# The order of matrix-product pieces on TensorE in a two-layer graph network kernel, and one PSUM read moved on VectorE

## The chip, the cores and the metric

The kernel runs on one core of a Trainium2 chip. The metric is device time in microseconds for one execution. Before the change it is 2293.26 us, the median of 3 runs (2292.56 to 2294.22).

## The reference: what is computed

The input x has 128 graphs of 128 nodes with 512 features. Two layers follow each other, each with a layer norm and a ReLU ahead of it and a residual sum behind it. All of it is in float32.

```python
h = relu(layernorm(x));  x = x + (norm_adj @ (h @ W0)) + b0
h = relu(layernorm(x))
q, k, v = h @ Wq + bq, h @ Wk + bk, h @ Wv + bv            # 8 heads of 64
attn = softmax(q k^T / 8 + (1 - adj) * -1e9)               # per graph and head
x = x + (attn @ v) @ Wo + bo
```

So there are five 512 x 512 weight products: W0, Wq, Wk, Wv and Wo.

## The kernel before, in words

Four graphs form a group, 32 groups in all. In the steady state a turn of the main loop (slot `t`) runs five blocks, named by a letter: W (the product with W0 for group t+1), Q, K, V (the products with Wq, Wk, Wv for group t) and Y (the product with Wo for group t-1). Each block is one `Projection` of seven steps, `n` = 0 to 6. Between the steps, and between the two halves of a step (`step(n)`, then `rest(n)`), a table called `plan` puts everything else: layer norms, transposes, scores, softmax, loads and stores. The schedule is manual: each engine works through its instructions in the order in which the program issues them. An instruction waits on semaphores for what it needs from other engines.

**Fewer multiplications.** A product of two 512 x 512 blocks is done in seven half-size products, P1 to P7 (the Winograd form of Strassen's scheme). Four of these, P2 to P5, are themselves split into seven pieces, each a 128 x 128 by 128 x 128 multiplication; P1, P6 and P7 are plain, four multiplications of 128 x 256 each. The sums of pieces are not made on TensorE: VectorE (in a few places ScalarE) reads each PSUM bank and adds it into the right blocks of the destination in SBUF.

**PSUM banks.** P1, P6 and P7 use one of the two `a` banks. P5 and later P3 use the two `d` banks: the seven pieces lie as four blocks in `d0` and three blocks in `d1` (`SEVEN`, `seven`, lines 403 to 411). P2 uses bank `b` and P4 bank `c`; each of the two is filled in three phases of 4, 2 and 1 pieces (`PHASES`, `phase`), because the sums allow a phase's places to be read, and then added to, by the next phase.

**The seven steps.** 0: P1. 1: P5 into `d0`, `d1`. 2: P2's phase of four into `b`. 3: P6. 4: P2's phase of two, then P3 into `d0`, `d1` on top of P5. 5: P7. 6: P2's last piece and P4's phase of four into `c`. P4's last two phases, of two pieces and of one, are put off: they go to a list, `tail`, and run within steps 1 and 2 of the following block. They are the trailing phases. Block K is an exception (`whole`): its P4 runs inside the block, with its first phase in step 4 ahead of P3, its second at the start of step 5, and its third in step 6. So W's trailing phases run in Q, Q's in K, V's in Y and Y's in W; V runs none.

**Reads on VectorE.** The bank of a phase is read by `read_phase`. The `d` banks are read by `read_seven`: part 0 reads the first two blocks of `d0` (in Q, K and V for P5 this is done by ScalarE), and then the first block of `d1` onto the diagonal; part 1 is four reads, the last of `d1` second and the last of `d0` fourth. Part 0 for P5 is issued in `rest(1)`, part 1 in `rest(2)`; for P3 both are in `rest(4)`. P3 writes on the same banks, so its first multiplication waits until P5 is read. Likewise a phase of `c` or `b` waits until the phase before it is read.

**What else stands in VectorE's queue.** The statistics of the layer norms (`BATCH_NORM_STATS2`, line 314) are put by the plan at "Q0b", "Q1b" and "Q3b" (the group's x just loaded) and at "K0b" and "K3b" (the second norm). "K3b" lies between P5's reads and those of step 4 in block K.

Of the kernel before, what the change touches and what calls it, by code (L numbers as in the profile page):

```python
# [29 lines left out]
P1, P5, P2, P6, P3, P7, P4 = PRODUCTS = (  # L30
    (A11, W11),
    (S1, T1),
    (A12, W21),
    (S2, T2),
    (S4, W22),
    (S3, T3),
    (A22, T4),
)
# [40 lines left out]
SEVEN = ((3, 6, 0, 0), (0, 5, 0, 1), (2, 3, 0, 2), (1, 0, 0, 3), (4, 4, 1, 0), (5, 2, 1, 1), (6, 1, 1, 2))  # L79
# [14 lines left out]
def kernel(  # L94
# [18 lines left out]
    P = 128  # L113
# [151 lines left out]


    INNER = [((T1, W22), step) for step in FIRST_RIGHT[:3]]
    INNER += [((W21, T4), WINOGRAD_RIGHT[0])]
    INNER += [((T1, W22), step) for step in FIRST_RIGHT[3:]]
    INNER += [((W21, T4), step) for step in WINOGRAD_RIGHT[1:]]  # L270

    def combine_inner(name, engine, steps=range(9)):
# [103 lines left out]
    class Projection:  # L376
# [23 lines left out]
                    else:  # L400
                        self.matmul(out[:, r], left[:, c, r, :], right[:, c, :], start)

        def seven(self, product, fresh):
            i, k = product
            for x, y, b, place in SEVEN:
                self.matmul(
                    bank[f"d{b}"][:, place * P : (place + 1) * P],
                    self.left.slot(i, x),
                    self.right.slot(k, y),
                    fresh and place == 0,  # L410
                )
# [35 lines left out]
        def read_seven(self, half, y, part, first=False):  # L447
            dst = self.cut(half, y)
            diagonal = self.diagonal(dst)
            m = [bank[f"d{b}"].rearrange("p (s f) -> p s f", f=P) for b in range(2)]  # L450
            columns = m[0][:, 0:2].unsqueeze(2).to_broadcast([P, 2, 2, P])
            if part == 1:
                self.add(dst[:, 1, 0], m[0][:, 3])
                self.add(diagonal, m[1][:, 1:3])
                self.add(dst[:, 0, 1], m[0][:, 2])
                self.add(diagonal, m[0][:, 2:4], ALU.subtract)
                return
            if first and self.first is not None:
                self.first(dst.rearrange("p j r f -> p r j f"), columns, y)
            else:  # L460
                self.add(dst.rearrange("p j r f -> p r j f"), columns)
            self.add(diagonal, m[1][:, 0:1].to_broadcast([P, 2, P]))

        def read_phase(self, half, y, src, n):
            dst, m = self.cut(half, y), src.rearrange("p (s f) -> p s f", f=P)
# [9 lines left out]
        def step(self, n):  # L475

            a, inner = bank[f"a{turn[0]}"], self.inner
            t, m = self.region(1, 0), bank["c"]
            left = tail.pop(0) if n in (1, 2) and tail else None
            if left:  # L480

                left[0]()
            if n == 0:
                self.left, self.right = self.a(), w_sb[self.w]
                self.product(a, P1, True)
                self.read_first(0, 0, a)
            elif n == 1:
                if inner:
                    self.seven(P5, True)
                else:  # L490
                    self.product(bank["d0"], P5, True)
            elif n == 2:
                if inner:
                    self.phase(bank["b"], P2, 0)
                else:
                    self.product(bank["b"], P2, True)
            elif n == 3:
                self.product(a, P6, False)
                self.read_first(0, 1, a)
            elif n == 4:  # L500
                if inner:
                    self.phase(bank["b"], P2, 1)
                    if self.whole:
                        self.phase(m, P4, 0)
                    self.seven(P3, False)
                    self.read_phase(0, 0, bank["b"], 1)
                    if self.whole:

                        self.whole(t[:, 0, :], m[:, : 2 * P], 0)
                        self.whole(t[:, 1, P:], m[:, 3 * P :], 1)  # L510
                        self.add(t[:, 0, :P], m[:, 2 * P : 3 * P])
                else:
                    self.product(bank["d0"], P3, False)
            elif n == 5 and self.whole:
                self.phase(m, P4, 1)
                self.product(a, P7, False)
                self.whole(t[:, 1, :P], m[:, 3 * P :], 1)
                self.add(t[:, 1, :P], m[:, :P])
                self.add(t[:, 0, :], a[:, : 2 * P])
                self.add(t[:, 1, P:], a[:, 3 * P :])  # L520
                turn[0] = 1 - turn[0]
            elif n == 5:
                self.product(a, P7, False)

                reads = [lambda: self.read_first(1, 0, a), lambda: self.read(1, 1, a)]
                for f in reads if self.stay else reads[::-1]:
                    f()
                turn[0] = 1 - turn[0]
            elif self.whole:
                self.phase(bank["b"], P2, 2)  # L530
                self.phase(m, P4, 2)
                self.read_phase(0, 0, bank["b"], 2)
                a = bank[f"a{1 - turn[0]}"]
                self.add(t[:, 1, :P], a[:, 2 * P : 3 * P])
                self.read(1, 1, a)
                self.read_phase(1, 0, m, 2)
            elif inner:
                self.phase(bank["b"], P2, 2)
                self.phase(bank["c"], P4, 0)
                self.read_phase(0, 0, bank["b"], 2)  # L540
                self.read_phase(1, 0, bank["c"], 0)
                for k in (1, 2):
                    tail.append(
                        (
                            lambda k=k: self.phase(bank["c"], P4, k),
                            lambda k=k: self.read_phase(1, 0, bank["c"], k),
                        )
                    )
            else:
                self.product(bank["c"], P4, True)  # L550
                self.read(1, 0, bank["c"])
            if left:
                left[1]()
            if n == 2:
                if inner:
                    self.read_phase(0, 0, bank["b"], 0)
                else:
                    self.read(0, 0, bank["b"])

        def rest(self, n):  # L560

            inner = self.inner
            if n == 1:
                if inner:
                    self.read_seven(1, 1, 0, True)
                else:
                    self.read_first(1, 1, bank["d0"])
            elif n == 2 and inner:
                self.read_seven(1, 1, 1)
            elif n == 4:  # L570
                if inner:
                    self.read_seven(0, 1, 0)
                    self.read_seven(0, 1, 1)
                else:
                    self.read(0, 1, bank["d0"])
# [272 lines left out]
    for t in range(-1, NG + 1):  # L848
# [3 lines left out]
        if 0 <= t - 1 < NG - 1:  # L852
            g = t - 1

            for first, final, place, f, *args in (
# [14 lines left out]
                place = first if t == 1 else final if last else place  # L870
# [307 lines left out]
```

## Time and profile before

| | |
|---|---|
| median of the runs | 2293.26 us |
| profiled execution, span from first to last instruction | 2291.6 us |
| TensorE busy with matmuls | 2273.9 us, 99% |
| weight loads on TensorE busy | 2132.9 us, 93% |
| VectorE busy | 1868.3 us, 82% |
| ScalarE busy | 1364.3 us, 60% |
| GpSimd busy | 1860.9 us, 81% |
| DMA, share of 16 engines | 80.6% |
| mean granted TensorE clock | 0.998 |

The profiled execution has no time of its own beside its span; the span lies 1.7 us below the median of the runs. A steady turn of the loop takes about 70 us. Matmul ends are modelled, so that overlapping records hide short gaps: the busy share of 99% does not say how much of the time TensorE waits. What counts are the starts. In an undisturbed stretch a 128 x 128 multiplication shows as two records whose starts lie 112 ns apart, and a 128 x 256 one as two records 216 ns apart. A weight load stands ahead of each record.

### The profile page before, as it was taken

The numbers are of one execution on the slowest core, as the hardware profiler recorded it, in microseconds if no ns is written. First come the engines' busy times: TensorE is split into PE (matmuls) and PEld (weight loads), VectorE is DVE, ScalarE is ACT, GpSimd is POOL, SyncE is SP. The second block draws the span as 40 slices with busy tenths as digits, with TensorE's granted clock in tenths as the row PEclk, the third lists the DMA queues.
The fourth block names the chain that finished last, engine by engine and source line by source line (L and its number), as shares of the span: only waits on it lengthen the run. The fifth ranks groups of instructions, "written<-read, shape, count | busy, mean of one in ns | idle before, by whom it ended". The sixth has DMA issues, their size and how long they took to land.

```text
span 2291.6 us, 50617 instructions
## 1 busy us (share of the span) xinstructions
PE 2273.9 (99%) x18151; PEld 2132.9 (93%) x18151; DVE 1868.3 (82%) x4832; ACT 1364.3 (60%) x3556; POOL 1860.9 (81%) x1927
## 2 busy tenths in 40 slices
PE   9899999999999999999999999999999999999999
PEld 8899999999999999999999999999999999999998
DVE  7877888888888788887888888888888888888876
ACT  3555565655656556656556565565665665655654
POOL 6899788878888788888888887879888888878854
PEclk9999999999999999999999999999999999999999
DMA  5388978889887889878898788998888987889872
GB/s 169 157 259 245 298 231 256 239 251 280 250 252 241 254 254 276 257 247 236 251 297 243 250 238 250 270 258 260 244 246 252 291 253 236 243 245 291 239 242 81
DMA packets 448587, 563.32 MB, mean 246 GB/s; under 512 B 326352, under 2 KB 333648, under 8 KB 447824
## 3 DMA queue, kind: packets, MB, share of 16 engines
q1 hardware_dynamic: 448336, 560.08, 80.6%
q8 instruction: 144, 2.36, 0.4%
q14 instruction: 107, 0.88, 0.1%
HBM read 358.68 MB, written 122.68 MB: 210 GB/s over the span
## 4 chain that ended last, share of the span: by engine, by line
PE 88%; POOL 3%; DMA 3%; DVE 3%; issue 1%; ACT 1%; SPq 0%; POOLq 0%; DVEq 0%; ACTq 0%
PE bank_a L388 31%; PE bank_d L388 19%; PE bank_c L388 10%; PE bank_b L388 10%; PE pa L605 5%; PE bank_d L754 3%; PE po L820 3%; DMA xt<-in_x_dram 2%; PE pss L754 1%; PE bank_b L820 1%; PE bank_a L820 1%; PE bank_b L754 1%; PE pt L674 1%; POOL xt L337 1%; DVE xt L429 1%
## 5 line engine op out<-in xcount | busy, mean ns | idle before, releaser
L781 ACT ACTIVATE att<-att,nmx 128x128 f32<-128x128 f32 x1024 | 396.3, 391 | 0.9 <-DVE nmx L773 0.9
L388 PE MATMUL bank_a<-op_h,w 128*128 128x256 f32 x1488 | 352.0, 379 | 0.0
L789 POOL TENSOR_TENSOR att<-att,rsm 128x1024 f32<-128x1024 f32 x128 | 242.7, 1897 | 82.3 <-DVE rsm L788 82.3
L388 PEld LDWEIGHTS bank_a<-op_h,w 128*128 128x128 f32 x1488 | 268.9, 190 | 29.0
L429 DVE TENSOR_TENSOR xt<-xt,bank_d 128x512 f32<-128x512 f32 x732 | 269.0, 416 | 19.0 <-DVE xt L429 0.9
L794 ACT COPY att<-att 128x2048 uint16<-128x2048 uint16 x121 | 229.3, 1895 | 66.0 <-POOL att L789 66.0
L333 ACT ACTIVATE h<-xt,nb,rs 128x512 f32<-128x512 f32 x254 | 207.2, 817 | 57.8 <-POOL nb L322 56.1
L711 ACT ACTIVATE q<-bank_a,bqk 128x256 f32<-128x256 f32 x192 | 80.4, 470 | 263.0 <-PE bank_a L388 263.0
L320 POOL TENSOR_TENSOR rs<-ve,mhalf 128x2 f32<-128x2 f32 (+1 forms) x129 | 91.4, 708 | 176.2 <-DVE ve L319 175.8
L388 PE MATMUL bank_d<-op_h,w 128*128 128x128 f32 (+1 forms) x1712 | 218.2, 279 | 0.7 <-issue 0.3
L90 POOL TENSOR_TENSOR op_o<-op_o 128x256 f32<-128x256 f32 x297 | 209.6, 729 | 10.0
L388 PEld LDWEIGHTS bank_d<-op_h,w 128*128 128x128 f32 x1712 | 204.0, 193 | 5.1 <-issue 3.1
L90 POOL TENSOR_TENSOR op_a<-op_a 128x256 f32<-128x256 f32 x279 | 196.8, 729 | 14.1 <-DVE op_a L365 4.5
L90 POOL TENSOR_TENSOR op_h<-op_h 128x256 f32<-128x256 f32 x270 | 190.4, 729 | 12.2 <-DVE op_h L365 2.9
L781 ACT ACTIVATION_READ_ACCUMULATOR att<-att,nmx 128x1 f32 x1024 | 194.1, 190 | 0.0
L314 DVE BATCH_NORM_STATS2 st<-xt 128x6 f32<-128x512 f32 x256 | 173.0, 676 | 18.4 <-DMA xt<-in_x_dram 18.3
L388 PE MATMUL bank_a<-w,op_o 128*128 128x256 f32 x768 | 181.7, 379 | 0.0
L388 PE MATMUL bank_a<-w,op_h 128*128 128x256 f32 x744 | 179.1, 384 | 0.0
L388 PE MATMUL bank_a<-w,op_a 128*128 128x256 f32 x744 | 176.1, 380 | 0.0
L439 DVE TENSOR_TENSOR xt<-bank_a,xt 128x512 f32<-128x512 f32 x252 | 167.2, 684 | 10.2 <-PE bank_a L388 2.7
L761 DVE SCALAR_TENSOR_TENSOR att<-bank_d,msk 128x512 f32<-128x512 f32 x128 | 82.5, 686 | 104.4 <-PE bank_d L754 96.8
L773 DVE TENSOR_REDUCE nmx<-att 128x8 f32<-128x1024 f32 x128 | 155.0, 1211 | 0.0
(188 smaller groups left out, 5944.3 us busy)
## 6 DMA issues: line engine op xcount, KB each, us to landing
w<-wd_v SPq DMA_DIRECT2D x93, 704.0 KB, 5.5
w<-wd_o SPq DMA_DIRECT2D x93, 704.0 KB, 6.8
w<-wd_q SPq DMA_DIRECT2D x90, 704.0 KB, 6.1
planes<-att SPq DMA_DIRECT2D x121, 512.0 KB, 4.5
w<-wd SPq DMA_DIRECT2D x87, 704.0 KB, 5.4
xt<-in_x_dram SPq DMA_DIRECT2D x63, 512.0 KB, 6.1
out_dram<-xt SPq DMA_DIRECT2D x62, 512.0 KB, 4.2
planes_h<-att SPq DMA_DIRECT2D x29, 512.0 KB, 3.0
```

Of the source, the lines that this page charges most:

```text
L90: engine.tensor_tensor(twice(out), twice(x), twice(y), ALU.subtract if minus else ALU.add)
L314: nc.vector.bn_stats(self.st[:, j, :], self.src[:, j, :])
L333: nc.scalar.activation(h, src[:, j, :], AF.Relu, bias=nb[:, j : j + 1], scale=rs[:, j : j + 1])
L388: nc.tensor.matmul(out, lhsT, rhs, start=start, stop=True, skip_group_check=True)
L429: nc.vector.tensor_tensor(dst, dst, src, f)
L439: nc.vector.tensor_tensor(t, src.rearrange("p (r f) -> p r f", r=2), t, ALU.add)
L605: nc.tensor.matmul(pa[:, c * P : (c + 1) * P], h[:, c * P : (c + 1) * P], ant, start=True, stop=True)
L754: nc.tensor.matmul(pss[p][:, c, :], qs[g][rows, c, cols], ks[g][rows, c, cols], start=True, stop=True)
L773: nc.vector.tensor_reduce(nmx, att_of(g, b), AX.X, ALU.max, negate=True)
L781: nc.scalar.activation(att[:, h, :], att[:, h, :], AF.Exp, bias=nmx[:, h : h + 1], scale=1.0, accum_out=sm[:, h : h + 1])
L789: nc.gpsimd.tensor_tensor(att, att, rsm.unsqueeze(2).to_broadcast([P, H, P]), ALU.mult)
L794: nc.scalar.copy(planes, halves)
```

## The change

The multiplications, reads and other instructions are the same in number and kind; their order on TensorE and VectorE is not. ScalarE, GpSimd and the DMA queue have the same order as before.

- Step 1: the trailing phase of two is moved from ahead of P5 to between P5's four pieces in `d0` and its three in `d1`.
- Step 2: the trailing phase of one is moved behind P2's phase of four. On VectorE its read goes behind the two reads of `b`.
- Step 4: P3 starts with its three pieces in `d1`; its four in `d0` follow.
- `read_seven`: the read of the first block of `d1` moves from the end of part 0 to the start of part 1. For P5 this takes it from `rest(1)` to `rest(2)`, behind the reads of `b` and of the trailing phase. For P3 both parts stand together, so nothing moves.

```diff
-        def seven(self, product, fresh):
+        def seven(self, product, fresh, banks=(0, 1)):
             i, k = product
-            for x, y, b, place in SEVEN:
+            for x, y, b, place in (s for c in banks for s in SEVEN if s[2] == c):
...
             if part == 1:
+                self.add(diagonal, m[1][:, 0:1].to_broadcast([P, 2, P]))
                 self.add(dst[:, 1, 0], m[0][:, 3])
...
                 self.add(dst.rearrange("p j r f -> p r j f"), columns)
-            self.add(diagonal, m[1][:, 0:1].to_broadcast([P, 2, P]))
...
             left = tail.pop(0) if n in (1, 2) and tail else None
-            if left:
-
-                left[0]()
...
             elif n == 1:
                 if inner:
-                    self.seven(P5, True)
+                    self.seven(P5, True, (0,))
                 else:
                     self.product(bank["d0"], P5, True)
+                if left:
+                    left[0]()
+                if inner:
+                    self.seven(P5, True, (1,))
             elif n == 2:
                 if inner:
                     self.phase(bank["b"], P2, 0)
                 else:
                     self.product(bank["b"], P2, True)
+                if left:
+                    left[0]()
...
-                    self.seven(P3, False)
+                    self.seven(P3, False, (1, 0))
...
-            if left:
-                left[1]()
             if n == 2:
                 if inner:
                     self.read_phase(0, 0, bank["b"], 0)
                 else:
                     self.read(0, 0, bank["b"])
+            if left:
+                left[1]()
```

Here `left` holds a trailing phase: `left[0]` its multiplications, `left[1]` its reads.

## The prediction, made before the changed kernel was run

> **What bounds the kernel now.** I read the page first, then the chain, the waits, and the timeline of single engines.
>
> ```profile
> PE 2273.9 (99%) x18151; PEld 2132.9 (93%) x18151; DVE 1868.3 (82%) x4832; ACT 1364.3 (60%) x3556; POOL 1860.9 (81%) x1927
> PE 88%; POOL 3%; DMA 3%; DVE 3%; issue 1%; ACT 1%; SPq 0%; POOLq 0%; DVEq 0%; ACTq 0%
> ```
>
> TensorE sets the end, and the same multiplications remain. So the change can only take away, or add, short stops of TensorE. The view of waits of the weight loads shows one large one:
>
> ```profile
> PEld bank_c L388 <- DVE xt L429: 10.9, 16, 4.2
> ```
>
> Most stops are too short for that view. I took the start of every matmul record from the timeline; where a bank changes, what the first two starts lie apart beyond 112 ns (216 ns for a wide record) is a stop. All such stops come to 44 us. By place: second trailing phase of W, in Q: 6.9 us in 16 turns. Second trailing phase of Y, in W: 4.5 in 29. First multiplication of P3: in Q 6.2, in V 4.1, in W 3.6, in Y 3.6, 30 turns each (0.12 to 0.14 us in one; in Q 0.26 in 16 turns). K's own second phase of P4: 5.6 in 28 (0.19 each). First trailing phase: 5.4 in 5. Each waits for VectorE's read of that bank.
>
> VectorE's queue in one Q block, where it starts late:
>
> ```profile
> 1875.90 0.69 DVE L314 BATCH_NORM_STATS2 st<-xt 128x6 f32<-128x512 f32 x1 [1.39 <-DMA xt<-in_x_dram]
> 1876.73 0.58 DVE L429 TENSOR_TENSOR xt<-xt,bank_c 128x128 f32<-128x128 f32 x2
> 1878.24 0.42 DVE L429 TENSOR_TENSOR q<-q,bank_d 128x256 f32<-128x256 f32 x1
> 1878.58 0.41 DVE L429 TENSOR_TENSOR xt<-xt,bank_c 128x256 f32<-128x256 f32 x1
> 1878.91 0.87 DVE L429 TENSOR_TENSOR q<-q,bank_b 128x256 f32<-128x256 f32 x2
> 1879.69 1.14 DVE L429 TENSOR_TENSOR q<-q,bank_d 128x128 f32<-128x128 f32 x4
> ```
>
> Statistics wait 1.39 us for x to land; the trailing phase's read behind them is late, and TensorE stops 0.81 us for it. The starts also give VectorE's pace: 0.34 us for a 256-wide read, 0.79 for the two of `b`, and 1.06 for the four of `d` (0.20, 0.33, 0.20, 0.33).
>
> In K the same queue decides a later stop:
>
> ```profile
> 1471.38 0.42 DVE L429 TENSOR_TENSOR q<-q,bank_c 128x256 f32<-128x256 f32 x1 [0.49 <-PE bank_c L388]
> 1472.28 0.87 DVE L429 TENSOR_TENSOR k<-k,bank_b 128x256 f32<-128x256 f32 x2 [0.47 <-PE bank_b L388]
> 1473.07 1.14 DVE L429 TENSOR_TENSOR k<-k,bank_d 128x128 f32<-128x128 f32 x4
> 1474.13 0.69 DVE L314 BATCH_NORM_STATS2 st<-xt 128x6 f32<-128x512 f32 x1
> ...
> 1475.94 0.60 DVE L429 TENSOR_TENSOR k<-k,bank_b 128x128 f32<-128x128 f32 x2
> 1476.46 0.28 DVE L429 TENSOR_TENSOR k<-k,bank_c 128x128 f32<-128x128 f32 x1
> ```
>
> ```profile
> 1475.04 1.64 PEld L388 LDWEIGHTS bank_d<-op_h,w 128*128 128x128 f32 x14
> 1476.80 0.52 PEld L388 LDWEIGHTS bank_c<-op_h,w 128*128 128x128 f32 x4
> ```
>
> From the read of `b` to the read of `c` VectorE never pauses. That last read ends at 1476.74; the weight load that waits for it starts 0.05 us later, where an undisturbed one would start 14 x 0.111 after 1475.04, at 1476.60.
>
> **What the Trainium skill says.** "PSUM — Partial Sum Buffer", section "Engine vs sequencer instructions": VectorE's queue is strictly first in, first out, and TensorE's matmuls keep program order while a weight load may overlap running ones. The trace agrees: the reads behind the 1.39 us wait are all late. "TensorE: Matmul & The Clock Gate", section "Step-by-step: what each phase is for": weights are pulled ahead of running matmuls. So it is here: a load starts 0.1 us ahead of its matmul, and after a stop the second start is some 0.1 us late as well, since that lead is lost; the 44 us count both. "VectorE: DVE Perf Modes", section "The DRAIN you can't avoid": the next operation waits for the pipe to drain, except where it is not held. Here reads of 0.42 us start 0.34 us apart, so the pace and not the duration is used.
>
> **The change part by part.** A multiplication takes two records, 0.223 us.
>
> *Trailing phases later.* In step 1 the first phase gets four multiplications ahead of it, 0.89 us of cover. The second phase keeps seven between it and the first, but its read now follows later work: where VectorE was late for another reason (x landing), TensorE reaches the wait 0.89 us later. Y's phases in W: all of 4.5 us goes. First phases: in the one of 4.0 us, 0.9 is filled; two at the end (0.7 and 0.5) go. I count 2.0 us. In Q's 16 late turns the stop here and the one at P3 are one debt, taken next.
>
> *P3's order and the moved read.* Before, VectorE needed, in Q, W and Y: `d1` (0.34), trailing (0.34), `b` (0.79), four of `d` (1.06), and P3 waited for the fourth. Now: `b`, trailing, `d1`, then `d`; P3's start waits for the second of these four only, the end of `d1`; `d0`'s wait comes 0.67 us after. Where VectorE is late throughout, P3 starts earlier by 0.53: from the first of these reads to the end of the last one wanted it was 0.34 + 0.34 + 0.79 + 0.20 + 0.33 + 0.20 + 0.41 = 2.61 us, and is 0.79 + 0.34 + 0.34 + 0.20 + 0.41 = 2.08. Of the 11 us in the 16 late turns of Q I take back 0.55 at most in each, and less where the debt is below that: 6.5 us.
>
> Where VectorE is on time, its chain starts when `b`'s phase ends, now 0.22 us earlier. Y at 1924: `b` from 1925.75, trailing 1926.54, `d1` 1926.88, `d` 1927.22 and 1927.42, ending 1927.83; plus 0.05 to the weight load: 1927.88, against 1927.84 undisturbed and 1927.96 before. So 0.05 of 0.12 us remains: W and Y gain 60 x 0.07 = 4.2; Q's 14 other turns 14 x 0.085 = 1.2. V has no trailing phase: `b` from 1421.43, `d1` 1422.22, `d` 1422.56, 1422.76, ending 1423.17, 1423.22 with the delay, ahead of the undisturbed 1423.29. V gains all, 4.1.
>
> *The price in K.* P3 is not late there (the first phase of P4 lies ahead of it). But two reads, 0.34 each, that filled VectorE's pauses of 0.49 and 0.47 us (and one wait for ScalarE) now stand behind `b`, in the unbroken chain to the read of `c`. It starts 0.22 earlier and is 0.68 longer: `b` 1472.06, trailing 1472.85, `d1` 1473.19, `d` 1473.53, statistics 1474.59, 0.46 later than before. All that follows is 0.46 later, and TensorE stops 0.65 instead of 0.19: 28 x 0.46 = 12.8 us lost. Only if VectorE had a pause left in this chain would it be less; it has none.
>
> *Waits added.* In Q the first piece of `d0` in P5 now carries three waits (VectorE, ScalarE, GpSimd) instead of two. The trace shows 0.04 us per three-wait start at the attention products: 30 x 0.04 = 1.2 us, at worst 4. GpSimd's operands are no new stop: those for Y at 1430 were finished at 1426.9. In step 4 the columns of `d0` can be read only at P3's end, up to 0.67 us later than now; this delays VectorE into the next block. There, P1 and four pieces of `d0` (2.6 us) cover it; without that cover it would be up to 0.4 us per block. No DMA is moved, and the queues of SyncE and GpSimd keep their order.
>
> Sum: 4.5 + 2.0 + 6.5 + 4.2 + 1.2 + 4.1 = 22.5 gained, 12.8 + 1.2 lost: 8.5 us net. The span goes from 2291.6 to about 2283; with the 1.7 us between span and median, **2284.8 us**.
>
> **Rivals.** *The price in K is not paid* (15%): then about 21 us gained, 2272. For it: K's chain rests on one engine's pace, measured in other orders. Against: its stop is 0.19 us in 28 turns alike, the mark of a chain without slack.
>
> *The gains at P3 are missing* (17%): a wait met 0.05 us late, now met twice (`d1`, then `d0`), costs 0.12 as before, by the lost lead. Then 9.5 us fall away in V, W, Y and on-time Q, and 13.0 gained stand against 14.0: 2294, no change. For it: my margins there are 0.07 us and less.
>
> *Slower: VectorE does not catch up between blocks* (13%). W and Y give VectorE some 10.6 us of reads in 11.6 us, and with reads of `d0` held back the next `b` is read late. By my sums VectorE is free 0.1 us before `b` in W and hardly at all in Q. Each 0.1 us of lateness stops TensorE 0.1 us at P3 in both, 60 blocks: 6 us. From 0.14 us the gain is used up; at 0.3 us it is 18 us, 2303.
>
> *Net as summed* (55%): 2279 to 2290, its own range from each term being off by a third.
>
> **How the numbers follow.** 0.2% is 4.6 us, about what can be told from no change: faster is below 2288.7, slower above 2297.8. Faster: the summed case in nine of eleven parts and the first rival, some 0.65; same: the rest of it, the second rival and a little of the third, 0.22; slower: 0.13. The range 2272 to 2296 leaves out most of the slower case and a tail beyond the first rival.
>
> **What would show it.** In K, the weight load of `c` about 0.65 us late in 28 turns, and its wait for VectorE's read of k among the longest of TensorE's, some 18 us. The wait of `bank_c` for xt shrunk from 10.9 us to 4 or less. P3's first load, now `d1`, undisturbed in V, and at most 0.05 late in W and Y. VectorE's waits for ScalarE in k and v (34.6 and 43.9 us) shrunk by about half or more, which alone is worth nothing. Wrong would be: no growth in K, or stops at `d0` in step 4.

## The result, and the profile after

The changed kernel takes 2307.49 us, the median of four runs (2306.1 to 2308.43), against 2292.91 for the kernel before on the same chip. The ratio is 1.0067, with a 95% interval from 1.0054 to 1.008: slower by 0.7%. The forecast was 2284.8 us, faster. The profiled execution spans 2305.9 us, 14.3 more than before, at a granted clock of 0.999.

The page of the changed kernel, the busy times and then the chain that ended last by engine:

```profile
PE 2258.2 (98%) x18151; PEld 2122.1 (92%) x18151; DVE 1863.4 (81%) x4832; ACT 1358.2 (59%) x3556; POOL 1861.5 (81%) x1927
PE 83%; DVE 11%; DMA 3%; POOL 1%; issue 1%; ACT 1%; SPq 0%; DVEq 0%; POOLq 0%; ACTq 0%
```

The number of instructions is the same and no engine is busier. But the chain now lies on VectorE for 11% of the span, where it was 3%, and on TensorE for 83%, where it was 88%. TensorE waits for VectorE more than before. The view of waits of the changed kernel (engine, line, what was waited for: us in total, times, longest) says where:

```profile
PEld bank_c L388 <- DVE k L429: 35.9, 30, 1.4
PE bank_c L388 <- DVE k L429: 30.0, 28, 1.2
...
PEld bank_d L388 <- DVE q L429: 5.1, 11, 0.7
...
PEld bank_c L388 <- DVE xt L429: 2.0, 4, 1.3
```

The wait of `bank_c` for VectorE's read of k is the second phase of P4 in K. The one for xt, the trailing phases, shrank from 10.9 us to 2.0. Measured by the starts of the records as in the prediction, the stops of TensorE are, in us:

| place | before | forecast | after |
|---|---|---|---|
| second phase of P4 in K (28 turns) | 5.6 | 18.4 | 37.4 |
| Q: W's second trailing phase, and P3's start | 13.1 | 5.4 | 9.9 |
| P3's start in V | 4.1 | 0 | 0.3 |
| P3's start in W and Y | 7.1 | 2.9 | 1.6 |
| Y's second trailing phase, in W | 4.5 | 0 | 0 |
| all others, first trailing phases and those inside runs of one bank too | 15.4 | 14.6 | 14.0 |
| sum | 49.7 | 41.2 | 63.2 |

The sum grew by 13.5 us, which is the 14.3 us of the span but for 0.8. Two rows miss the forecast: K by 19 us and Q by 4.5.

So the question is why the stop in K is 1.34 us in each turn and not 0.65. VectorE's part of one turn of K in the changed kernel (start us, busy us, engine, line, operation, out <- in):

```profile
1482.98 0.68 DVE L314 BATCH_NORM_STATS2 st<-xt 128x6 f32<-128x512 f32 x1
1483.70 0.18 DVE L315 BATCH_NORM_AGGREGATE mv<-st 128x2 f32<-128x6 f32 x1
1483.80 0.66 DVE L314 BATCH_NORM_STATS2 st<-xt 128x6 f32<-128x512 f32 x1
1484.50 0.18 DVE L315 BATCH_NORM_AGGREGATE mv<-st 128x2 f32<-128x6 f32 x1
1484.71 0.74 DVE L319 TENSOR_SCALAR ve<-mv 128x2 f32<-128x2 f32 x1
1485.36 0.59 DVE L429 TENSOR_TENSOR k<-k,bank_b 128x128 f32<-128x128 f32 x2
1485.88 0.28 DVE L429 TENSOR_TENSOR k<-k,bank_c 128x128 f32<-128x128 f32 x1
```

GpSimd in the same stretch:

```profile
1482.81 1.27 POOL L364 TENSOR_TENSOR op_a<-op_a 128x512 f32<-128x512 f32 x1
1484.16 1.27 POOL L365 TENSOR_TENSOR op_a<-op_a 128x512 f32<-128x512 f32 x1
```

And TensorE's weight loads:

```profile
1483.31 1.64 PEld L388 LDWEIGHTS bank_d<-op_h,w 128*128 128x128 f32 x14
1486.21 0.52 PEld L388 LDWEIGHTS bank_c<-op_h,w 128*128 128x128 f32 x4 [1.26 <-DVE k L429]
```

The layer norm's scale instruction (`ve<-mv`, line 319) has two numbers per partition to add an epsilon to, and takes 0.74 us. It starts 0.55 us into GpSimd's last combining operation (line 365, 1484.16 to 1485.42) and ends 25 ns after it. In the kernel before the same pair looks like this. VectorE:

```profile
1475.87 0.17 DVE L319 TENSOR_SCALAR ve<-mv 128x2 f32<-128x2 f32 x1
```

GpSimd:

```profile
1474.54 1.27 POOL L364 TENSOR_TENSOR op_a<-op_a 128x512 f32<-128x512 f32 x1
1475.89 1.27 POOL L365 TENSOR_TENSOR op_a<-op_a 128x512 f32<-128x512 f32 x1
```

There it starts about 20 ns ahead of line 365, in the short gap after line 364, and takes 0.17 us. This is so in 27 of 29 turns, 11 to 28 ns ahead (the median duration in K is 170 ns before and 734 ns after). In the changed kernel it ends 23 to 28 ns behind the end of a GpSimd operation in every one of 29 turns, whether it lasts 0.38 or 1.18 us. The statistics beside it, which also lie inside GpSimd's operations, keep their 0.66 to 0.68 us.

The Trainium skill, page "SBUF — State Buffer", section "Who interferes with whom", says that VectorE and GpSimd share a pair of SBUF ports as an exclusive lock; that `tensor_scalar` is among the forms that can take it, when its operands meet the conditions of a mode with two ports; and that whichever issues first holds it for the whole instruction while the other fully blocks. What the trace shows for this instruction agrees: 0.17 us ahead of GpSimd's operation, and until its end, plus 25 ns, behind its start. The other direction shows too, though it is small: in the kernel before, line 365 lasts 1.27 us (the median) where VectorE's instruction starts 24 ns ahead of it, and 1.29 us where it starts 11 to 13 ns ahead. The experiments ask whether this is the cause.

### The profile page after: what moved, and what is told of

It reads as the page before. It is cut to its first block, busy times and chain, and to the rows that moved or that the text cites. A ratio compares the mean times of both kernels' runs of the same rounds, so it can differ in the third digit from the quotient of the medians.

```text
span 2305.9 us, 50528 instructions
## 1 busy us (share of the span) xinstructions
PE 2258.2 (98%) x18151; PEld 2122.1 (92%) x18151; DVE 1863.4 (81%) x4832; ACT 1358.2 (59%) x3556; POOL 1861.5 (81%) x1927
## 4 chain that ended last, share of the span: by engine, by line
PE 83%; DVE 11%; DMA 3%; POOL 1%; issue 1%; ACT 1%; SPq 0%; DVEq 0%; POOLq 0%; ACTq 0%
PE bank_a L388 30%; PE bank_d L388 18%; PE bank_b L388 9%; PE bank_c L388 9%; PE pa L608 5%; DVE k L429 4%; DMA xt<-in_x_dram 3%; PE bank_d L757 3%; PE po L823 3%; DVE st L314 2%; PE pt L677 1%; PE pss L757 1%; PE bank_b L823 1%; PE bank_a L823 1%; DVE xt L429 1%; DVE q L429 1%
## 5 line engine op out<-in xcount | busy, mean ns | idle before, releaser
L429 DVE TENSOR_TENSOR xt<-xt,bank_d 128x512 f32<-128x512 f32 x732 | 263.2, 414 | 13.3 <-PE bank_d L388 11.2
L388 PE MATMUL bank_d<-op_h,w 128*128 128x128 f32 (+1 forms) x1712 | 227.7, 279 | 4.5 <-DVE q L429 2.9
L388 PEld LDWEIGHTS bank_d<-op_h,w 128*128 128x128 f32 x1712 | 210.0, 192 | 11.3 <-DVE q L429 5.1
L388 PE MATMUL bank_c<-op_h,w 128*128 128x128 f32 (+1 forms) x856 | 130.0, 280 | 30.1 <-DVE k L429 30.0
```

Of the source, the lines that this page charges most:

```text
L388: nc.tensor.matmul(out, lhsT, rhs, start=start, stop=True, skip_group_check=True)
L429: nc.vector.tensor_tensor(dst, dst, src, f)
```

## The experiments

**Theory 1**: the predicted shift of 0.46 us in VectorE's chain pushes the scale instruction behind the start of GpSimd's operation; it then lasts until that ends, and all reads behind it are late. **Theory 2**: VectorE's chain keeps its durations, and a shift costs itself alone. Each run is compared with runs of the kernel before on the same chip, whose medians are 2291.57, 2291.74 and 2291.87 us.

**K as before.** The changed kernel, with K alone in its old order:

```diff
             left = tail.pop(0) if n in (1, 2) and tail else None
+            late = not self.whole
+            if left and not late:
+                left[0]()
...
-                    self.seven(P3, False, (1, 0))
+                    self.seven(P3, False, (1, 0) if late else (0, 1))
...
-            if left:
+            if left and late:
                 left[1]()
```

(and the same condition at the other `left` calls and at the moved read).

> The kernel after, but in block K (the one whose P4 runs inside it) the order of before, on TensorE and VectorE: trailing phases ahead, d0 ahead of d1 in P3, the read of d1's first block with part 0. Both theories put the whole loss into K: its stop returns to 0.19 us, and 32 us go from the kernel after: 2275 us, some 18 us below the kernel before. If the loss were elsewhere (P3 split over two waits, VectorE late between blocks) it would stay near 2307 us.

Measured: 2273.76 us against 2291.57 before; ratio 0.9919 [0.9904, 0.9934]. K's stop is 5.3 us again and V, W and Y keep their gains. The loss of the change lies in K; without it the change is a gain of 18 us.

**The scale instruction later.** The changed kernel, but in K the scale instruction stands behind the reads that TensorE waits for:

```diff
-            at(t, "K3b" if g < NG - 1 else "Q3b", ln2, g, 1)
+            if g < NG - 1:
+                at(t, "K3b", ln2, g, 1, (0, 1), ())
+                at(t, "K5b", ln2, g, 1, (), (0, 1))
+            else:
+                at(t, "Q3b", ln2, g, 1)
```

> The kernel after, with the scale instruction of K3b (and the two GpSimd steps behind it) issued two steps later, behind step 5 of K, out of the chain to the read of c. Theory 1: K's stop falls from 1.34 us by the 0.57 us that the instruction waited and by its own pitch of 0.3: to about 0.5 us, 28 x 0.87 = 24 us faster than the kernel after, 2283 us. Theory 2: only the 0.3 us go, 8 us, 2299 us.

Measured: 2286.44 us; ratio 0.998 [0.9971, 0.9988]. K's stop is 16.1 us, 0.58 in a turn. One tiny instruction moved takes 21 us of stops, and some 20 us of time, off the changed kernel. This takes away its 0.74 us and also the 0.22 us between the aggregate and it, so it doesn't yet say why it was long.

**A short delay, first try.** The kernel before, with a memset of one column ahead of the scale instruction in K:

```diff
+                at(t, "K3b", ln2, g, 1, (0, 1), ())
+                at(t, "K3b", nc.vector.memset, warm, 0.0)
+                at(t, "K3b", ln2, g, 1, (), (0, 1))
```

> The kernel before, with one more VectorE instruction in block K, turns 1 to 29: a memset of one column, some 0.06 us, between the statistics at K3b and the small scale instruction (line 319) behind them. Theory 1 (that scale instruction may not run while a GpSimd operation on SBUF runs, and waits for its end; before, it just fits the gap between two): it now comes 20 to 60 ns too late, waits about 1.2 us for GpSimd's last combining operation, shows as 1.2 to 1.4 us long instead of 0.17, and K's stop of TensorE at the second phase of P4 grows from 0.19 to about 1.4 us: 28 x 1.25 = 35 us slower, 2328 us. Theory 2 (VectorE's queue only gets longer by the reads put into it): 28 x 0.06 = 1.7 us slower, 2295 us.

Measured: 2292.16 us; ratio 1.0 [0.9991, 1.0008]. Neither number came, because there was no delay: the memset (59 ns) ran within the 0.22 us in which VectorE waits between the aggregate and the scale instruction, which still started some 20 ns ahead of line 365. It told nothing.

**A real delay.** The kernel before, with 128 columns of statistics made once more, ahead of the others:

```diff
+    spare = const.tile([P, 6], F32, name="spare")
...
+                at(t, "K3b", lambda g=g: nc.vector.bn_stats(spare, xts[g, 1][:, 0, 0:P]))
                 at(t, "K3b", ln2, g, 1)
```

> The kernel before, with one thing added: in K, ahead of the second norm's statistics, VectorE makes the statistics of 128 columns once more into a spare tile (worked out from 0.69 us for 512 columns: about 0.2 us). No product and no read is moved. The short delay is meant to push VectorE's scale instruction (128 x 2) past the start of GpSimd's last combining operation (1.27 us). Theory 1 (the scale instruction, once behind that start, lasts until the operation's end): it lasts 1.0 to 1.2 us in place of 0.17, K's stop at the second phase of P4 grows from 0.19 to 1.2 to 1.4 us, 28 x 1.1 = 31 us: about 2323 us. Theory 2 (VectorE's chain keeps its durations, and a delay costs only itself): 28 x 0.2 = 5.6 us: about 2298 us.

Measured: 2324.57 us against 2291.74; ratio 1.0143 [1.0129, 1.0157]. VectorE and then GpSimd in one turn of it:

```profile
1423.25 0.29 DVE L901 BATCH_NORM_STATS2 spare<-xt 128x6 f32<-128x128 f32 x1
1423.45 0.68 DVE L315 BATCH_NORM_STATS2 st<-xt 128x6 f32<-128x512 f32 x1
...
1425.17 1.13 DVE L320 TENSOR_SCALAR ve<-mv 128x2 f32<-128x2 f32 x1
```

```profile
1425.01 1.27 POOL L366 TENSOR_TENSOR op_a<-op_a 128x512 f32<-128x512 f32 x1
```

The added instruction costs 0.20 us from start to start. The scale instruction now starts 0.16 us behind GpSimd's operation (one line further down in this kernel) and lasts 1.13 us. K's stop is 36.5 us, 1.30 in a turn. 0.2 us of work, 28 times, cost 33 us. Theory 2's 2298 is out.

**Another form in the same place.** The changed kernel; only the scale instruction in K has another form:

```diff
+            if plain:
+                nc.vector.tensor_reduce(self.ve[:, c], self.mv[:, c, 1:2], AX.X, ALU.add)
+            else:
                 nc.vector.tensor_scalar(self.ve[:, c], self.mv[:, c, 1], EPS, None, ALU.add)
```

> The changed kernel, all orders as they are, and one instruction in K of another form: the second norm's scale instruction (TENSOR_SCALAR, 128 x 2) is a TENSOR_REDUCE over one element, 128 x 2 too, in the same place of VectorE's queue and with the same wait. It leaves out the addition of epsilon in this one norm half. Theory 1 (the form of the instruction shuts it out while GpSimd's combining operation runs): the reduce lasts 0.2 us or less where TENSOR_SCALAR lasted 0.74, K's stop goes from 1.34 to 0.75 to 0.8 us (the predicted 0.65 and 0.14 of slower reads of b), 28 x 0.56 = 15.8 us less: about 2291 us. Theory 2 (any VectorE instruction that stands there is held, by its place or by a wait that it carries): 2307 us as in the changed kernel.

Measured: 2292.73 us against 2291.87; ratio 1.0005 [0.9999, 1.0012], where the changed kernel's is 1.0067: some 14 us less. The instruction's own row (duration min/median/max in ns) in this kernel:

```profile
L320 DVE TENSOR_REDUCE ve<-mv x29: 154/155/157, 134.7 to 2107.1; 128x2 f32<-128x2 f32 x29
```

It starts as far inside GpSimd's operation as before (0.556 us, the median of both kernels) and lasts 0.155 us in all 29 turns. K's stop is 22.1 us, 0.79 in a turn. So neither the place nor a wait made the instruction long, but its form while GpSimd worked: 37.4 less 22.1 makes 15.3 us. The other 0.14 of the 0.79 us has another cause: the predicted 0.65 took the two reads of `b` to follow each other as before, but in K and Q the second now starts 0.53 us after the first instead of 0.45, and in K the first starts 0.11 after `b` is done instead of 0.04. In the turn of the changed kernel shown above:

```profile
1480.40 0.95 DVE L429 TENSOR_TENSOR k<-k,bank_b 128x256 f32<-128x256 f32 x2 [1.92 <-PE bank_b L388]
```

In the kernel before the pair takes 0.87 us. The trace shows what has come in between. Before, each of the two reads waited for one engine (TensorE, then VectorE's own first read). The first block of `d1` used to be read ahead of them; now they are the first to follow ScalarE's part 0, and both wait for ScalarE too. For the additional wait an instruction of its own (EVENT_SEMAPHORE, 21 ns) stands ahead of each read, and each starts 0.07 us later: 0.14 in all. In V only the first read has the additional wait, and only the first is later (0.11 us after `b`, the second 0.46 after it); W and Y have none and keep their 0.46. Where only the read is moved (below), K and Q show the same 0.53; where only the trailing phases are, 0.45. So the moved read brings it, and it goes with the additional waits in every block looked at; no run took a wait away by itself.

**One part alone: the trailing phases.** Against the kernel before:

```diff
-            if left:
-                left[0]()
...
-                    self.seven(P5, True)
+                    self.seven(P5, True, (0,))
...
+                if left:
+                    left[0]()
+                if inner:
+                    self.seven(P5, True, (1,))
...
+                if left:
+                    left[0]()
...
+            if left:
+                left[1]()
```

> The kernel before with the trailing phases moved later (on TensorE and in VectorE's order), and nothing else: P3 in the old order, the read of d1's first block in its old place. In K the chain from b to the scale instruction is 0.12 us longer (a read of 0.34 in it, a start 0.22 earlier), perhaps 0.2. Theory 1: that is enough to put the scale instruction inside GpSimd's last combining operation; it waits about 1.1 us; K's stop is about 1.4 us, 35 us lost; with 13 us gained at the trailing phases and some 9 us lost at P3 it ends near 2324 us. Theory 2: K loses 28 x 0.15 = 4 us, and it ends near 2293 us.

Measured: 2333.38 us; ratio 1.0179 [1.0164, 1.0194]. The scale instruction starts 0.09 us behind line 365 and lasts 1.20 us; K's stop is 36.2 us. The trailing stops of Q and W are nearly gone, but P3's start, still in `d0`, costs 18.6 us in Q, 9.0 in W and 6.9 in Y. That is 21 us more than before where the expectation had some 9, which is why the time lies 9 us above theory 1's 2324; theory 2's 2293 is out.

**One part alone: the read.** Against the kernel before:

```diff
             if part == 1:
+                self.add(diagonal, m[1][:, 0:1].to_broadcast([P, 2, P]))
...
-            self.add(diagonal, m[1][:, 0:1].to_broadcast([P, 2, P]))
```

> The kernel before, with the read of d1's first block moved from ahead of the reads of b to behind them, and nothing else: P3 starts in d0 and waits for the last of the four reads of part 1, now 0.34 us later. Theory 1: stops at P3 grow by 0.34 us in 120 blocks, 41 us, and K's chain is 0.34 us later, which puts the scale instruction 0.3 us behind the start of GpSimd's operation, so that it lasts about 1.1 us and K's stop grows from 0.19 to 1.3 to 1.5 us, 28 x 1.2 = 34 us: about 2368 us. Theory 2 (the chain keeps its durations): 41 + 28 x 0.34 = 50.5 us more, about 2343 us.

Measured: 2363.17 us; ratio 1.0319 [1.0302, 1.0336], nearer theory 1's 2368 than theory 2's 2343. K's stop is 37.3 us, the scale instruction 0.84 us long (it starts 0.45 behind line 365). P3's starts cost 61.8 us in place of 17.4, while W's trailing stop in Q fell from 6.9 to 1.0.

K's stop is thus 1.29, 1.30, 1.33 and 1.34 us in four kernels whose chain was moved by four different amounts: where the scale instruction ends is set by GpSimd and not by VectorE.

**One part alone: P3's order.** Against the kernel before:

```diff
-                    self.seven(P3, False)
+                    self.seven(P3, False, (1, 0))
```

> The kernel before, with P3's three pieces in d1 ahead of its four in d0 and nothing else; the read of d1's first block and the trailing phases stay where they were. The gain at P3's start that the prediction spoke of should be there alone: V 4.1, W 3.6 and Y 3.6 us of stops go, and 2 to 6 of Q's 6.2; K's stop stays 5.6 us, and the scale instruction in K stays 0.17 us. Theory 1: 13 to 17 us less, about 2277 us. Rival (the gains at P3 in the changed kernel come from the moved trailing phases and read, and not from the order of the banks): less than 5 us, 2287 us or more.

Measured: 2298.62 us against 2291.74; ratio 1.0028 [1.0016, 1.004]. Both expectations missed. All 17.4 us at P3's start are gone, Q's too, so the order of the banks is indeed what gains them. But other stops came in their place. The view of waits of this kernel:

```profile
PEld bank_c L388 <- DVE xt L429: 38.1, 96, 4.1
```

Y's trailing phase in W, TensorE's weight loads and then VectorE:

```profile
1441.80 1.60 PEld L388 LDWEIGHTS bank_a<-w,op_a 128*128 128x128 f32 x8
1443.83 0.52 PEld L388 LDWEIGHTS bank_c<-w,op_o 128*128 128x128 f32 x4 [0.43 <-DVE xt L429]
```

```profile
1441.38 1.28 DVE L439 TENSOR_TENSOR xt<-bank_a,xt 128x512 f32<-128x512 f32 x2
1442.58 0.41 DVE L429 TENSOR_TENSOR xt<-xt,bank_b 128x256 f32<-128x256 f32 x1
1442.91 0.87 DVE L429 TENSOR_TENSOR xt<-xt,bank_c 128x256 f32<-128x256 f32 x2
```

The columns of `d0` come last in P3 and are read first. VectorE is late into the next block, and the first trailing phase waits there for the read of `c`: 0.30 us in a steady turn of W and of Q; in K the third phase of P4, in step 6, waits 0.18. New stops of 22 us stand against 17 gained. The prediction had named this cost, "up to 0.4 us per block" without the cover of four pieces of `d0`; here the trailing phase is not moved and the cover is missing. P3's order needs the moved trailing phases.

**A better version.** K as before, and the scale instruction in K later:

> The changed kernel with K in the order of the kernel before, and the second norm's scale instruction in K taken out of VectorE's chain (from K3b to K5b). Theory 1 (the scale instruction is part of the chain that makes K's stop, also where it lasts only 0.17 us and follows 0.2 us of waiting): K's stop of 5.3 us goes, about 2268.5 us against 2273.8 with K as before alone. Theory 2 (it costs nothing as long as it lies ahead of GpSimd's operation): 2273.8 us.

Measured: 2268.93 us against 2291.74; ratio 0.9899 [0.9885, 0.9912]. K's stop is gone from the list of stops. This is faster than both kernels, by 1.0% than the kernel before. Even at 0.17 us the scale instruction, with the 0.22 us of waiting ahead of it, was what made K's old stop of 0.19.

**The read back, with K as before.** The read of the first block of `d1` in its old place in all blocks; the edit is shown against the kernel with K as before:

```diff
             if part == 1:
-                if not self.whole:
-                    self.add(diagonal, m[1][:, 0:1].to_broadcast([P, 2, P]))
...
-            if self.whole:
-                self.add(diagonal, m[1][:, 0:1].to_broadcast([P, 2, P]))
+            self.add(diagonal, m[1][:, 0:1].to_broadcast([P, 2, P]))
```

> The changed kernel with K in the order of the kernel before, and in all blocks the read of d1's first block back ahead of the reads of b; the trailing phases and P3's order stay changed. Theory 1 (VectorE has a pause ahead of b that this read fills, so that the chain from b to P3 is 0.34 us shorter): the 1.6 us of stops at P3 in W and Y and some of the 9.1 us in Q go, 2270 to 2272 us against 2273.8 with the read moved. Rival (the read ahead of b delays b, and with it P2's second phase and P3): 1 to 4 us more, 2275 to 2278 us.

Measured: 2274.95 us; ratio 0.9925 [0.9912, 0.9937], not to be told from 0.9919 with the read moved. Stops at P3 in W and Y fall from 1.7 to 0.4 us and in Q from 9.2 to 5.6, as theory 1 had it, but 4.5 us of new ones appear in Q where P2's second phase waits for the reads of `b`, as the rival had it. With K as before and P3 starting in `d1`, the read's place makes no difference that these runs can tell.

## Why the prediction was wrong

*The step that failed is "The price in K".* Its first half was right in kind: two reads of 0.34 us come into a chain without a pause, and all behind them is later. Its second half, "TensorE stops 0.65 instead of 0.19", summed the chain with durations and starts from the kernel before. Two of them did not survive the shift. The first and larger one is the scale instruction, whose 0.17 us became 0.74. That is 28 x 0.56 = 15.8 us by the trace, and 15.3 us of stops and some 14 us of time by the run with another form. The second is the reads of `b`: with their additional waits the statistics stand 0.58 us later against P3's start (the median), not 0.46, and the stop without the long scale instruction is 0.79, not 0.65: 28 x 0.14 = 3.9 us. "Waits added" counted those of TensorE alone and put VectorE's at nothing. Together the two are the 19 us by which K misses. (The 1.2 us charged there for TensorE in Q did not come: P5's first piece starts without a stop in 29 of 30 turns.)

*It could have been read before.* The row of line 319 in the kernel before (min/median/max in ns):

```profile
L319 DVE TENSOR_SCALAR ve<-mv x129: 153/170/958, 4.9 to 2164.0; 128x2 f32<-128x2 f32 x127, 128x1 f32<-128x1 f32 x2
```

An instruction of 128 x 2 that takes 170 ns in the median and once 958 has been held up. Nine of the 129 there are longer than 0.2 us, and each ends 24 to 29 ns behind the end of a GpSimd operation. The prediction looked at VectorE's queue alone, and wrote that it would be cheaper only if a pause were left; that it could be dearer was not asked. None of its rivals had this mechanism; the slower one, VectorE late between blocks, is not what happened.

*Q: sizes were off.* Forecast were 7.7 us of gains, and 3.2 came. The 16 late turns gave 5.8 us instead of 6.5. But x doesn't land late in the same turns in both traces: in four of the other 14 it is late in the changed kernel alone (VectorE waits 0.88 to 1.42 us for it), and they cost 2.2 us more. In the turns in which x lands in time the stop at P3 was 0.136 us (14 turns) and is 0.167 (19 turns); the forecast had it fall to 0.05. In one such turn, VectorE in the changed kernel:

```profile
1818.77 0.29 DVE L429 TENSOR_TENSOR xt<-xt,bank_c 128x128 f32<-128x128 f32 x1
1818.97 0.69 DVE L314 BATCH_NORM_STATS2 st<-xt 128x6 f32<-128x512 f32 x1
...
1820.08 0.95 DVE L429 TENSOR_TENSOR q<-q,bank_b 128x256 f32<-128x256 f32 x2
```

and P3's weight loads:

```profile
1822.27 1.64 PEld L388 LDWEIGHTS bank_d<-op_h,w 128*128 128x128 f32 x14
```

The same two in the kernel before, VectorE:

```profile
1805.85 0.69 DVE L314 BATCH_NORM_STATS2 st<-xt 128x6 f32<-128x512 f32 x1
```

and the weight loads that begin P3:

```profile
1809.89 1.19 PEld L388 LDWEIGHTS bank_d<-op_h,w 128*128 128x128 f32 x10
```

The last statistics ahead of `b` stand 3.30 us ahead of P3 where they stood 4.04; without the two stops (0.167 and 0.134) they are 0.77 later. They are queued behind the trailing phase's read, and the change puts that phase 0.89 us later. VectorE so comes to `b` with no pause, and the reads of `b` are slower too, as in K. The prediction had counted the trailing phase's move as cover only, and not the statistics behind its read. This is read from the trace; no run took it apart.

*Right were* V (3.7 of 4.1 us), W and Y at P3 (5.5 against 4.2), Y's second trailing phase (all of 4.5), the first trailing phases (some 1.9 of 2.0; in the first turn of Q the stop of 4.0 became two, of 1.7 at P5's start and 1.4) and the cover in step 4: the stops at the start of a block that the order of P3 alone brings are not there in the changed kernel; that run shows what they would have cost. With K set aside, the changed kernel gains 18 us where the prediction's sum without K was 21.3.

## What to carry to other kernels

A chain's durations hold only where the other engines stand as they did: before a shift is summed, look at what the instructions of the shifted chain will newly overlap with, and above all at small VectorE instructions beside long GpSimd ones. A row whose maximum is many times its minimum was the sign here; where its shortest and its longest instructions stood beside GpSimd told the cause. A tiny instruction that nobody on the critical path needs should not stand in front of a read that TensorE waits for.

## What the runs showed of the hardware

- VectorE's TENSOR_SCALAR of 128 x 2 in float32 from SBUF to SBUF, started 0.07 to 0.91 us inside a GpSimd TENSOR_TENSOR of 128 x 512, ended 21 to 28 ns after that one's end in every such turn of K in the changed kernel and in three experiments; it took 0.38 to 1.2 us instead of 0.17. Started about 20 ns ahead of it, it took 0.17 us.
- Started 11 to 13 ns ahead, it made GpSimd's operation some 0.015 us longer (1.29 us) than when it started 24 ns ahead (1.27 us).
- A TENSOR_REDUCE of 128 x 2 in the same place took 0.155 us in 29 of 29 turns, and BATCH_NORM_STATS2 inside such GpSimd operations kept its 0.66 to 0.69 us. In this place the form of the instruction decided.
- A VectorE read of `b` with a second engine to wait for has an EVENT_SEMAPHORE of 21 ns ahead of it and started 0.07 us later than one without.
- VectorE has 0.217 us between the start of the last aggregate and that of the scale instruction that needs it; a memset of 59 ns placed there was free.
